# Four key tiles of values at a time: twelve tiles of logits and three buffers of streamed weights

## The chip, the cores and the metric

The kernel runs on one core of a Trainium2 chip. The time is what the device takes for one execution, in microseconds (us), as a median over runs. The engines of the core are named as in the profile: PE is TensorE (matmuls), PEld its weight loads, DVE is VectorE, ACT is ScalarE, POOL is GpSimd, and SP is the engine whose queue issues the DMAs.

## What is computed

The input is x, eight images of 512 channels and 32x32 pixels in float32. Layer 0 is group normalization followed by a block with two attention bottlenecks, added to x; layer 1 is group normalization followed by a 1x1 convolution with a masked weight and a permutation of its channels, added again. Cut to what matters here:

```
t  = silu(bn(conv1x1(gn(x))))                    # 512 -> 512, in two halves of 256
ys = [t[:, :256], t[:, 256:]]
for i in range(2):
    z = silu(bn(conv3x3(ys[-1])))                # 256 -> 256
    q, k, v = conv1x1(z)                         # 4 heads of 64 channels, 1024 pixels
    logits = q^T (k + r) / 8                     # 1024 x 1024 for every head
    z = softmax(logits) v
    z = silu(bn(conv1x1(z)))
    ys.append(ys[-1] + z)
x = x + silu(bn(conv1x1(concat(ys))))            # 1024 -> 512
x = x + permuted_masked_conv1x1(gn(x))           # 512 -> 512
```

All matmuls are in float32. The trace shows two PE instructions for each of them (one for a transpose).

## The kernel before

The attention is cut into 64 **units**: eight images, two bottlenecks, two pairs of heads, two halves of the 1024 queries. Within a unit the 1024 keys lie in eight **key tiles** of 128. For each key tile t a unit does the following steps, which are methods of the class `Unit`:

- `logits(t)` (L487): two matmuls, one for each head of the pair, each into a PSUM bank of its own. Each uses 64 of the 128 rows of the array, so that the two run side by side. ScalarE copies both banks into an SBUF tile `st` of 128x1024 (L500), and VectorE keeps a running maximum `mx` straight from the banks (L505).
- `top` and `spread` (L507, L516): once per unit, transposes on TensorE (`mt`, `mb`) turn the running maximum into the negated maximum of each query, spread over all partitions.
- `soften(t)` (L523): VectorE adds that maximum to `st` (L525), ScalarE takes the exponential in place (L526), GpSimd adds the tile to the running sum of the denominator (L531).
- `values(t)` (L533): two matmuls, one for each head, each into 64 of the 128 columns of the array, again side by side, accumulated over all eight key tiles into one PSUM bank `po` (L537).
- `finish` and `divide` (L545, L554): the denominators (`den`), their reciprocals, and the division of `po` into `q`.

The loop over units (L1003 to L1034) is a software pipeline written out by hand. While a unit's tiles are softened and its values are taken, the logits of the next unit are made. A pass of the inner loop handles two key tiles, t and t+1: soften both, take the values of the two tiles of the pass before, make the next unit's logits of t and t+1, and then let `advance` put in a share of the **filler**, the work of all other stages. The filler of a slot of four units is the 3x3 convolution of a coming bottleneck (`m<-plane`, L297), its projection to q, k and v (`qk`, `v`, L175 and L389), and a background list of 1x1 convolutions (`cv<-x`, `cv<-y`, `l<-x`, `m<-q`, all at L175). Each filler matmul uses the whole 128x128 array. Its results are taken out of PSUM by ScalarE or VectorE. The shares that `advance` hands out are counted in estimated costs, so that the filler falls at the same place of a unit whatever the values do.

What the change and the prediction touch:

- PSUM has eight banks: two for `mb` (pool `ps_m`), one for `po` (`ps_o`), and five (`ps_f`, L63) that logits, filler, `mt` and `den` share. Two key tiles of logits take four of these five.
- The pool `stp` (L53) holds ten tiles `st`: the eight of the unit that is softened and two for the next unit's logits. The logits of the third key tile go where the first tile of the current unit was, so that their copy comes after the values and the sum of that tile.
- `wp` (L54) has four buffers of streamed weights (6 KB a partition each), `wt` (L60) three temporaries of the transform before the 3x3 convolution.
- Nearly all DMAs are issued by the one queue of SP, in an order that the scheduler of the tile framework writes when the kernel is built. It also orders each engine's instructions. VectorE's order of softening, maximum and transform is held by `in_turn` (L182).
- `bn_sb`, `s_sb`, `rw_sb` and `rh_sb` (L86 to L89) hold small parameters, and `tri` (L658) a triangular matrix; each has SBUF of its own.

Of the kernel before, what the change touches and what calls it, by code (L numbers as in the profile page):

```python
# [15 lines left out]
F32 = mybir.dt.float32  # L16
# [6 lines left out]
P = 128  # L23
NB = 8
CT = 4
IT = 2
F = 32
HW = F * F
HALF = 512
NBLK = 2  # L30
HD = 64
NG = 16
KT = 8
NGR = 17

BN_CV1, BN_CV2, BN_M1, BN_M2, BN_ALL = 0, 4, 8, 12, 16
# [3 lines left out]
def conv_preact_kernel(ctx: ExitStack, tc: tile.TileContext, x, cv1, cv2, mcv1, qkv, mcv2, bn, rw, rh, conv, s_in, t_in, out):  # L40
# [3 lines left out]
    def pool(name, bufs, **kw):  # L44
        return ctx.enter_context(tc.tile_pool(name=name, bufs=bufs, **kw))

    const = pool("const", 1)
    dram = pool("dram", 1, space=bass.MemoryType.DRAM)
    small = pool("small", 2)
    qp = pool("qp", 2)  # L50
    kp_ = pool("kvp", 3)
    stp = pool("stp", 10)
    one = pool("one", 1)  # L53
    wp = pool("wp", 4)  # L54
    gx = pool("gx", 4)
    wm = pool("wm", 1)
    gy = pool("gy", 4)
    gr = pool("gr", 2)
    tp = pool("tp", 3)
    wt = pool("wt", 3)  # L60
    ps_m = pool("ps_m", 1, space=PSUM)
    ps_o = pool("ps_o", 1, space=PSUM)
    ps_f = pool("ps_f", 5, space=PSUM)  # L63
# [7 lines left out]
    def half_tile(name):  # L71
        return tp.tile([P, HALF], F32, tag="t", name=name)
# [10 lines left out]
        return t  # L83


    bn_sb = const.tile([P, 4, BN_ALL], F32, name="bn_sb")  # L86
    s_sb = const.tile([P, 2, CT, NG], F32, name="s_sb")
    rw_sb = const.tile([P, NBLK, IT, F], F32, name="rw_sb")
    rh_sb = const.tile([P, NBLK, IT, F], F32, name="rh_sb")  # L89


    w_m1 = [[dram.tile([P, IT, IT, 3, P], F32, name=f"w_m1_{i}_{r}") for r in range(6)] for i in range(NBLK)]
# [515 lines left out]
    def last_weights():  # L608
# [46 lines left out]

        yield

        tri = small.tile([P, P], F32, tag="tri", bufs=1, name="tri")  # L658
        nc.gpsimd.affine_select(
            out=tri, in_=ones, pattern=[[1, P]], compare_op=ALU.is_gt, fill=0.0, base=0, channel_multiplier=-1  # L660
        )
# [28 lines left out]
        for i in range(CT):  # L690
# [5 lines left out]
            t = half_tile(f"wl_{i}")  # L696
# [35 lines left out]
    clock = Clock()  # L732
# [138 lines left out]
    def slot_filler(s):  # L871

        prev = slots[s - 1] if s else (None, 0)
        nxt = slots[s + 1] if s + 1 < len(slots) else (None, 0)
        todo, needed = [], 0.0

        def add(us, g):
            nonlocal needed
            todo.append((us, g))
            needed += us  # L880

        im, i = nxt
        add(8.0, bg.take(8.0))
        if im and i == 1:
            add(7.0, im.conv_m2(0))
            add(0.0, call(im.transform, 1, 3.0, 1.0))
            add(9.0, bg.take(9.0))
        products = im.conv3(i) if im else iter(())
        if prev[1] == 1:
            if im:  # L890
                add(21.3, (us for _, us in zip(range(16), products)))
            add(7.0, prev[0].conv_m2(1))
            add(0.0, call(lambda: finishing(prev[0])))
        if im:
            add(10.7 if prev[1] == 1 else 32.0, products)
            add(7.0, bg.take(7.0))
        if im:
            add(21.0, im.project(i))
        if s + 2 < len(slots) and slots[s + 2][1] == 0:
            add(0.0, call(slots[s + 2][0].load_y))  # L900
            add(0.0, call(slots[s + 2][0].transform, 0, 8.0, 1.3))
        rest = SHARE - needed if im else 70.0
        if rest > 0:
            todo.append((rest, bg.take(rest, wait=True)))
        total = sum(c for c, _ in todo)
        return needed, total, todo
# [36 lines left out]
    first, second = images[:2]  # L943
# [16 lines left out]
    bg.prepare()  # L960
    first.transform(0, 0.0, 0.0)
    side = last_weights()
    for n, us in enumerate(first.conv3(0)):
        clock.tick(us)
# [16 lines left out]
    for s in range(len(slots)):  # L981
        needed, total, todo = slot_filler(s)
        state = {"done": 0.0}

        def filler():
            for us, g in todo:
                start = state["done"]
                for cost in g:
                    clock.tick(cost)
                    state["done"] += cost  # L990
                    yield

                state["done"] = max(state["done"], start + us)

        fill = filler()

        def advance(share):
            goal = max(share * total, min(1.0, share / 0.74) * needed + 0.1)
            while state["done"] < goal:
                if next(fill, "end") == "end":  # L1000
                    break

        steps = 4 * (KT + 2)  # L1003
        for j in range(4):
            u = units[4 * s + j]
            nxt = units[4 * s + j + 1] if 4 * s + j + 1 < len(units) else None
            base = j * (KT + 2)
            u.top()
            clock.tick(0.9)
            advance((base + 1) / steps)  # L1010
            u.spread()
            clock.tick(0.9)
            advance((base + 2) / steps)
            if before:
                before.finish()
                clock.tick(0.9)
            for t in range(0, KT, 2):
                u.soften(t)
                if before and t == 0:
                    before.divide(1)  # L1020
                u.soften(t + 1)
                if t:
                    u.values(t - 2)
                    u.values(t - 1)
                    clock.tick(2.0)
                if nxt:
                    nxt.logits(t)
                    nxt.logits(t + 1)
                    clock.tick(2.0)
                advance((base + 4 + t) / steps)  # L1030
            u.values(KT - 2)
            u.values(KT - 1)
            clock.tick(2.0)
            before = u  # L1034
        for _ in fill:
            pass
# [59 lines left out]
```

## Time and profile before

| what | time |
|---|---|
| median of three runs | 3276.86 us (3268.33 to 3284.32) |
| the profiled execution | 3278.47 us |
| its span, first to last instruction | 3276.7 us |
| PE busy | 3159.1 us, 96% of the span |
| DVE busy | 2045.9 us, 62% |
| ACT busy | 1756.6 us, 54% |
| POOL busy | 1219.1 us, 37% |
| mean granted TensorE clock | 0.990 |

The profiled execution lies 1.61 us above the median, and its span 1.8 us below its own time. A unit takes about 3276.7 / 64 = 51.2 us. A group of instructions in the profile is named by engine, line, the tile written and the tiles read. A matmul's form is given as rows by columns of the array: 128\*128 for the filler, 64\*128 for logits (`lg`), 128\*64 for values (`po`). Matmuls overlap in the pipeline, so that their listed durations are longer than the distance from one start to the next; the distance is what the stream costs. An idle time is put down to the engine whose result ended it.

### The profile page before, as it was taken

Reading aid. Unit: us, or ns where it says so; the run is one execution under the profiler, and the core shown is the slowest. Engines: PE = TensorE matmul, PEld = TensorE weight load, DVE = VectorE, ACT = ScalarE, POOL = GpSimd, SP = SyncE. Lnnn points to the kernel's source line nnn. Section 1 sums busy time; section 2 is a strip of 40 time slices with the busy share of each in tenths; the row PEclk is TensorE's granted clock in tenths of the full one; section 3 lists DMA queues with packets and bytes.
Section 4 is the critical chain, followed back from the end, with each engine's and each line's share of the span. In section 5 each row is a group of like instructions: output and inputs, shape, how many; then the busy total and the mean of one; then the engine's idle time right before and its main releaser. Section 6 shows DMA issues by size and latency. Waiting matters only on the chain.

```text
span 3276.7 us, 33257 instructions
## 1 busy us (share of the span) xinstructions
PE 3159.1 (96%) x11716; PEld 1538.0 (47%) x11716; DVE 2045.9 (62%) x2717; ACT 1756.6 (54%) x2369; POOL 1219.1 (37%) x971
## 2 busy tenths in 40 slices
PE   7999999998999999999999999999999999999998
PEld 3645345353545445354545445354445444453343
DVE  5436566666666575767666675767656676666642
ACT  3245765854545655644545555644655554646631
POOL 2104433335334343344334343444334433444420
PEclk9999999999999999999999999999999999999999
DMA  8752352330323241423323341423333341423366
GB/s 292 275 171 71 119 170 94 116 106 20 121 98 106 75 148 55 161 84 106 122 98 105 104 144 54 161 84 108 124 105 108 101 141 49 160 71 116 111 217 205
DMA packets 142007, 399.30 MB, mean 122 GB/s; under 512 B 13072, under 2 KB 14352, under 8 KB 141840
## 3 DMA queue, kind: packets, MB, share of 16 engines
q1 hardware_dynamic: 141120, 396.94, 36.1%
q8 instruction: 93, 1.52, 0.2%
q14 instruction: 74, 0.61, 0.1%
q10 hardware_dynamic: 720, 0.23, 0.0%
HBM read 317.42 MB, written 79.69 MB: 121 GB/s over the span
## 4 chain that ended last, share of the span: by engine, by line
PE 69%; DVE 11%; issue 5%; ACT 4%; DMA 4%; POOL 1%; POOLq 0%; SPq 0%; ACTq 0%; DVEq 0%
PE cv L175 14%; PE m L297 12%; PE po L537 11%; PE lg L494 10%; PE qk L175 6%; PE l L175 5%; PE v L389 3%; DVE st L525 3%; PE mt L513 2%; PE m L175 2%; DVE rb L556 2%; DVE mx L505 2%; PE den L549 2%; PE mb L521 2%; DMA x<-in_x 1%
## 5 line engine op out<-in xcount | busy, mean ns | idle before, releaser
L531 POOL TENSOR_TENSOR sum<-sum,st 128x512 f32<-128x512 f32 x768 | 973.9, 1299 | 771.5 <-ACT st L526 771.5
L526 ACT ACTIVATE st<-st 128x1024 f32<-128x1024 f32 x512 | 534.3, 1056 | 471.4 <-DVE st L525 464.8
L505 DVE TENSOR_TENSOR mx<-mx,lg 128x512 f32<-128x512 f32 x768 | 479.3, 681 | 434.1 <-ACT st L500 433.6
L500 ACT COPY st<-lg 128x512 f32<-128x512 f32 x1024 | 528.1, 594 | 246.1 <-PE lg L494 189.9
L525 DVE TENSOR_TENSOR st<-st,mb 128x1024 f32<-128x1024 f32 x512 | 604.2, 1213 | 79.8 <-PE mb L521 79.8
L297 PE MATMUL m<-plane,w_m 128*128 128x256 f32 x2304 | 534.0, 386 | 18.0 <-DVE z L351 8.3
L494 PE MATMUL lg<-q,k 64*128 64x512 f32 x2048 | 534.6, 618 | 10.4 <-ACT rb L551 3.3
L537 PE MATMUL po<-st,v 128*64 128x512 f32 x2048 | 509.5, 609 | 17.2 <-ACT st L526 11.4
L297 PEld LDWEIGHTS m<-plane,w_m 128*128 128x128 f32 x2304 | 431.4, 191 | 142.7 <-issue 40.8
L531 POOL TENSOR_TENSOR sum<-st,st 128x512 f32<-128x512 f32 x128 | 162.2, 1288 | 834.1 <-ACT st L526 712.0
L175 PE MATMUL cv<-y,w_cv 128*128 128x512 f32 x1024 | 466.5, 600 | 4.9 <-DVE mx L505 2.1
L494 PEld LDWEIGHTS lg<-q,k 64*128 64x128 f32 x2048 | 188.9, 186 | 346.2 <-issue 236.5
L175 PEld LDWEIGHTS cv<-y,w_cv 128*128 128x128 f32 x1024 | 185.5, 190 | 252.0 <-issue 231.6
L537 PEld LDWEIGHTS po<-st,v 128*64 128x64 f32 x2048 | 125.2, 136 | 327.6 <-issue 231.6
L556 DVE RECIPROCAL rb<-rb 128x256 f32<-128x256 f32 x128 | 216.1, 1725 | 66.0 <-ACT rb L551 66.0
L175 PE MATMUL cv<-x,w_cv 128*128 128x512 f32 x512 | 242.2, 622 | 12.3 <-DVE mx L505 4.1
L175 PE MATMUL l<-x,w_l 128*128 128x512 f32 x512 | 235.2, 604 | 9.6 <-DVE mx L505 6.2
L175 PE MATMUL qk<-z,w_qkv 128*128 128x512 f32 x512 | 234.2, 600 | 1.6 <-DVE mx L505 1.6
L514 DVE TENSOR_REDUCE nm<-mt 128x4 f32<-128x512 f32 x128 | 83.0, 685 | 221.5 <-PE mt L513 221.2
L130 ACT ACT_TABLE_LOAD x122 | 156.5, 1283 | 14.7 <-PE m L175 6.4
L175 PEld LDWEIGHTS cv<-x,w_cv 128*128 128x128 f32 x512 | 97.0, 197 | 138.7 <-issue 112.1
L175 PEld LDWEIGHTS l<-x,w_l 128*128 128x128 f32 x512 | 93.3, 191 | 133.6 <-issue 106.5
(144 smaller groups left out, 2342.1 us busy)
## 6 DMA issues: line engine op xcount, KB each, us to landing
w_m<-w_m SPq DMA_DIRECT2D x96, 768.0 KB, 4.4
w_cv<-in_cv SPq DMA_DIRECT2D x90, 512.0 KB, 3.5
y<-y SPq DMA_DIRECT2D x64, 512.0 KB, 4.7
x<-in_x SPq DMA_DIRECT2D x56, 512.0 KB, 5.2
y<-y SPq DMA_DIRECT2D x64, 256.0 KB, 3.6
k<-r SPq DMA_DIRECT2D x32, 512.0 KB, 3.8
res<-y SPq DMA_DIRECT2D x32, 512.0 KB, 4.2
xr<-in_x SPq DMA_DIRECT2D x32, 512.0 KB, 4.3
```

Of the source, the lines that this page charges most:

```text
L130: nc.scalar.activation(dst, src, AF.Silu, bias=bn_b[:, col : col + 1], scale=bn_s[:, col : col + 1])
L175: nc.tensor.matmul(ps, w, moving, start=(n == 0), stop=(n == len(terms) - 1))
L297: nc.tensor.matmul(ps[:, ts(co, 256)].rearrange("p (t x) -> p t x", x=F), w[:, co, c, dx], u[:, 9 * c : 9 * c + 8, dx : dx + F], start=(j ...
L389: nc.tensor.matmul(ps[:, ts(j, P)], z[:, c, ts(4 * j4 + j, P)], w[:, c, 512 + P * hp : 512 + P * hp + P], start=(c == 0), stop=(c == IT - 1),)
L494: nc.tensor.matmul(lg[h], self.k[r, ts(t, P)], self.q[r, self.hp, ts(self.half, HALF)], start=True, stop=True)
L500: nc.scalar.copy(st[:, h], lg[h])
L505: in_turn(nc.vector.tensor_tensor(self.mx[:, h], so_far[:, h], lg[h], ALU.max))
L525: in_turn(nc.vector.tensor_tensor(st, st, flat(self.mb), ALU.add))
L526: nc.scalar.activation(st, st, AF.Exp)
L531: nc.gpsimd.tensor_tensor(self.acc[:, h], so_far[:, h], self.st[t][:, h], ALU.add)
L537: nc.tensor.matmul(self.po[HD * h : HD * h + HD], self.v[:, t, ts(h, HD)], self.st[t][:, h], start=(t == 0), stop=(t == KT - 1),)
L556: nc.vector.reciprocal(self.rb[:, r], self.rb[:, r])
```

## The change

The values of four key tiles are taken together: tiles 0 to 3 in the pass t = 4, ahead of the next unit's logits of tiles 4 and 5, and tiles 4 to 7 after the last pass. The passes t = 2 and t = 6 have no values. So that the next unit's logits of four key tiles find a place before the first values are taken, `stp` has twelve tiles. The 8 KB come from one weight buffer (`wp` 3), one temporary (`wt` 2), and from the small parameters and `tri`, which now share one buffer of the keys' pool `kvp` at the start. All edits, with blank lines left out:

```diff
-    stp = pool("stp", 10)
+    stp = pool("stp", 12)
-    wp = pool("wp", 4)
+    wp = pool("wp", 3)
-    wt = pool("wt", 3)
+    wt = pool("wt", 2)
...
-    bn_sb = const.tile([P, 4, BN_ALL], F32, name="bn_sb")
-    s_sb = const.tile([P, 2, CT, NG], F32, name="s_sb")
-    rw_sb = const.tile([P, NBLK, IT, F], F32, name="rw_sb")
-    rh_sb = const.tile([P, NBLK, IT, F], F32, name="rh_sb")
+    par = kp_.tile([P, HW], F32, tag="k", name="par")
+    def param(first, shape):
+        return par[:, first : first + P].rearrange("p (a b c) -> p a b c", b=shape[0], c=shape[1])
+    s_sb = param(0, (CT, NG))
+    rw_sb = param(128, (IT, F))
+    rh_sb = param(256, (IT, F))
+    bn_sb = par[:, 512 : 512 + 4 * BN_ALL].rearrange("p (a b) -> p a b", b=BN_ALL)
...
-        tri = small.tile([P, P], F32, tag="tri", bufs=1, name="tri")
+        tri = par[:, 384:512]
...
                 u.soften(t + 1)
-                if t:
-                    u.values(t - 2)
-                    u.values(t - 1)
-                    clock.tick(2.0)
+                if t == KT // 2:
+                    for key in range(KT // 2):
+                        u.values(key)
+                    clock.tick(4.0)
                 if nxt:
                     nxt.logits(t)
                     nxt.logits(t + 1)
                     clock.tick(2.0)
                 advance((base + 4 + t) / steps)
-            u.values(KT - 2)
-            u.values(KT - 1)
-            clock.tick(2.0)
+            for key in range(KT // 2, KT):
+                u.values(key)
+            clock.tick(4.0)
```

## The prediction, on record before the run

> **What bounds the kernel now.** I read the busy table first, then the chain of waits in one unit, then who waited for whom, then VectorE's and SP's timelines around the places that the change moves.
>
> The busy table:
>
> ```profile
> PE 3159.1 (96%) x11716; PEld 1538.0 (47%) x11716; DVE 2045.9 (62%) x2717; ACT 1756.6 (54%) x2369; POOL 1219.1 (37%) x971
> ```
>
> TensorE is nearly always busy, so the time is TensorE's work plus the few waits in it. The change can gain only in what the stream itself costs, or in those waits. The chain of waits in 1224 to 1250 us shows the stream (start, duration, what):
>
> ```profile
> 1224.63 1.87 PE po L537 x8
> 1226.49 1.92 PE lg L494 x8
> 1228.41 5.38 PE m L297 x24
> 1233.79 1.87 PE po L537 x8
> 1235.66 1.92 PE lg L494 x8
> 1237.58 5.38 PE m L297 x24
> 1242.95 1.87 PE po L537 x8
> 1244.82 1.97 PE lg L494 x8
> ...
> 1247.03 0.57 ACT st L500
> ...
> 1247.63 0.70 DVE mx L505
> ...
> 1248.37 1.78 PE m L297 x7
> ```
>
> Two things are to be seen. A group of values (po, two key tiles) takes 1.87 us. Full-array matmuls of 512 columns follow each other every 0.43 us (24 of the kind `cv<-x` run from 152.21 to 162.51 us, 0.429 each), and eight half-array ones, two abreast, fill four such places: 1.72 us. So each group costs 0.15 us for changing the form. And at the end the filler (m at 1248.37) waits for a bank: logits, then ScalarE's copy, then VectorE's maximum. That is the chain which paces TensorE where it waits at all.
>
> Waits of all engines, and TensorE's alone (total us, times, longest):
>
> ```profile
> DVE mx L505 <- ACT st L500: 446.9, 185, 9.2
> ACT st L500 <- PE lg L494: 189.9, 98, 7.3
> ```
>
> ```profile
> PE po L537 <- ACT st L526: 11.4, 6, 4.4
> PE mt L513 <- DVE mx L505: 10.7, 3, 3.6
> ...
> PE po L537 <- DVE q L558: 5.8, 8, 0.9
> ```
>
> ScalarE's copies wait for TensorE's logits only 98 times, of some 256 pairs of key tiles; otherwise ScalarE or VectorE is late and TensorE ahead. TensorE's waits are small because its stream is spaced widely enough. VectorE in the same stretch:
>
> ```profile
> 1237.44 2.48 DVE L505 TENSOR_TENSOR mx<-mx,lg 128x512 f32<-128x512 f32 x4 [4.27 <-ACT st L500]
> ...
> 1243.69 2.34 DVE L525 TENSOR_TENSOR st<-st,mb 128x1024 f32<-128x1024 f32 x2
> 1247.63 2.48 DVE L505 TENSOR_TENSOR mx<-mx,lg 128x512 f32<-128x512 f32 x4 [1.60 <-ACT st L500]
> ```
>
> One pass costs VectorE 2.34 (soften two tiles), 1.60 (last exponential and first copy on ScalarE) and 2.48 (four maxima): 6.4 us in a row, and its filler work on top (here six operations between 1239.84 and 1243.77, 3.9 us). TensorE's pass takes 1.87 + 1.92 + 5.38 = 9.2 us.
>
> **The change, part by part.**
>
> *Form changes removed.* Two groups of four places, joined, lose one 0.15 us (0.14 by the step to the next group within rounding; I take 0.14). Two joints a unit in 64 units would be 128. The order of instructions in the two built programs has 947 changes of form before and 834 after, 113 fewer, because the scheduler still splits some groups. 113 x 0.14 = **-16 us**, all on the path, since TensorE is the path. Ends: 113 x 0.09 (a bare change: 0.52 instead of 0.43 us between starts at a border) = -10, and 128 x 0.15 = -19.
>
> *Logits come earlier in the passes t = 2 and t = 6.* Without the values ahead of them, the next unit's logits of these passes, and the filler behind them, start 1.87 us earlier; TensorE's pass is then 7.3 us, against VectorE's 6.4 plus filler work. What is late next is the five shared banks. In the shown pass, the filler at 1248.37 waits for a bank whose maximum ended at 1248.33. That maximum hangs on the softening at 1243.69, which stands behind VectorE's work for the 3x3 convolution and not behind the logits. Logits at 1242.95 instead of 1244.82 don't free it sooner: TensorE stops for about 1.87 us, and the values that had filled this time are still to be done later. So there the whole 1.87 is lost. In the pass that starts at 1224.63 the filler's next bank was free 0.62 us before its need, and 1.87 - 0.62 = 1.25 is lost.
>
> I did this for all 63 units that have a next one, from the trace's semaphore events: for every TensorE instruction between the group that goes and the next group, how long before its start its last input or bank had come, letting ScalarE and VectorE move up where their own inputs and predecessors permit. What is short of 1.87 us is lost. For t = 2, 43 of 63 units lose, together 49 us; for t = 6, 25 of 63, 35 us. The upper end is +84 us, the lower end 0.
>
> Three things make it less. (a) In the new program ScalarE copies the logits of these passes ahead of the second exponential more often: the third key tile in 36 units instead of 24, the seventh in 16 instead of 5. Each brings the maximum forward by one exponential (1.06 us): 23 x 1.06 = -24 us at best, and I take it. (b) A unit that stopped at t = 2 is later at t = 6 and finds VectorE further on; mean loss 49/63 = 0.8 us, for the some 25 units with a loss at t = 6, in the four tenths of them where the copy does not wait for TensorE at the fifth tile: -7 us. (c) Waits of TensorE elsewhere shrink: values wait for exponentials (11.4), for the division (5.8: the first values now stand one pass later), transposes for the last maximum (10.7). Of these 28 us I take two thirds, -18; ends 0 and -28. Together 84 - 24 - 7 - 18 = **+35 us**.
>
> The copies that waited for the sums of GpSimd (41.3 us, 18 times) and for values (14.4, 7 times) because the tile was not free lose that wait with twelve tiles. ScalarE is not the bound, so I cost this at nothing; the bound is inside (c).
>
> *The rule and the row.* The Trainium skill, page "TensorEngine Tiling (Array Packing)", says in Key Properties that a change of tiling mode drains TensorE, which the 0.15 us show. Its section PSUM Bottleneck says that tiling speeds up the matmuls but not the emptying of PSUM, which speaks against this change. It gives no duration for either. By that rule alone none of the 84 us would come back, and the sum would be 68 us slower.
>
> *Weights in three buffers instead of four.* A load is issued when the buffer comes free, a use later than before. SP's timeline:
>
> ```profile
> 1379.11 0.42 SPq L78 DMA_DIRECT2D w_m<-w_m  x1
> ...
> 1398.57 11.22 SPq L78 DMA_DIRECT2D w_m<-w_m  x2
> ```
>
> The weights issued at 1379.11 are first used at 1409.3. With three buffers, one of them held by a background convolution, they would be issued when the product two before ends, at 1398.5, land some 4.4 us later (the median of these loads) or 7.4 at worst, and still be 3.4 us early. Over all loads the margin before use is 5 us or more with three buffers, outside four places like this one. What stands behind the load on SP's in-order queue moves too: walking the new order of the queue with the old release times, only two weights near 160 us, where TensorE does nothing but filler, land late (3.8 us, one wait), and two image tiles by about 1 us. **+4 us**, ends 0 and +8.
>
> *The rest.* Two temporaries instead of three: all their writers and readers but the last are VectorE's, in order; nothing. The parameters in a buffer of the keys: used only until 160 us, before the third key tile of keys is loaded; nothing. Twelve tiles at the start let weights' raw pieces load earlier, on a stretch where TensorE already runs: nothing.
>
> *Sum.* -16 + 35 + 4 = +23 us on the profiled 3278.5, which is 1.6 above the median: **3300 us** against 3276.9.
>
> **Rivals.**
>
> - *TensorE keeps its pace, faster.* If VectorE, which idles 38% of the span, follows the earlier logits, the losses at t = 2 and t = 6 stay under some 15 us and only -16 and -18 remain: 3250 us or so, at best 3277 - 16 - 28 = 3233. For it: 38 of 63 units have no loss at t = 6. Against it: the copies wait for TensorE in only 98 cases. It decides where the banks' losses, after (a) and (b), are below 18 us.
> - *It cancels, no change.* Losses of 18 to 50 us, against the same gains: 3260 to 3293. One step of mine, (a) or (c), being twice as good suffices.
> - *All is lost.* Nothing of the 84 comes back: 3277 - 16 + 84 + 8 = 3353.
> - *Weights become the bound.* The queue's head waits longer with three buffers and holds up image loads and stores. For it: SP waits mostly for buffers of weights. Against it: margins above. Price: 4 to 5 us for each late load, 30 late loads for 4%; I give it little.
> - *It doesn't do what it says.* The scheduler could split the groups again; the order shows 15 of 128 joints missing, which is counted.
>
> **How the numbers follow.** Measurements of this kernel tell about 0.5% (16 us) from no change. Forecast, slower by over 0.5%, with all-lost and weights: 0.45 + 0.08 + 0.03; cancels 0.24; TensorE keeps its pace 0.20. The range reaches from a little above the best case, 3245, to a little below the worst, 3345; the likeliest case's own range is 3293 to 3325.
>
> **What would show it.** Right: groups of 16 values in a row with 3.58 us or so; fewer form changes; TensorE's waits for `mx` (filler after the third and seventh logits) up by some 40 us, those of values for exponentials down; the waits of copies for GpSimd's sums gone. Wrong: if waits for `mx` don't grow, VectorE followed; if waits for DMAs appear on PE, the weights were the matter; if the busy share of VectorE's chain moves forward by more than an exponential, my static margins were too strict.

## The result, and the profile after

The changed kernel takes 3289.75 us (median of nine runs, 3282.92 to 3301.72), against 3277.7 us for the kernel before on the same chip. The ratio is 1.0038, with a 95% interval of 1.0022 to 1.0053: slower by 0.38%, some 12 us. The profiled execution took 3292.98 us, with a span of 3291.0 us.

The busy table after:

```profile
PE 3168.4 (96%) x11716; PEld 1550.7 (47%) x11716; DVE 2036.6 (62%) x2717; ACT 1757.5 (53%) x2371; POOL 1217.1 (37%) x971
```

TensorE is still the path, with the same number of instructions and more time. The chain of waits around the same work as before (the middle of a 3x3 convolution):

```profile
1227.58 6.67 PE m L303 x30
1234.25 1.92 PE lg L500 x8
1236.17 1.49 PE m L303 x6
...
1237.68 4.15 PE m L303 x18
1241.83 3.58 PE po L543 x16
1245.41 1.11 PE lg L500 x4
...
1253.53 2.26 DVE st L531 x2
1255.79 0.61 DVE mx L511
...
1256.45 4.15 PE m L303 x18
```

The joint is there: 16 values in a row take 3.58 us, where two groups took 2 x 1.87 = 3.74. What a joint saves is some 0.15 us. And the chain leaves TensorE for longer before the filler at 1256.45 gets its bank: from 1246.52 to 1256.45, almost all of it on VectorE (the maximum of the logits before, filler work, softening, the next maximum), where before it left TensorE for 1.6 us. Such a stretch is not lost as a whole: TensorE had other work meanwhile and stood idle for 0.32 us of it. TensorE's own waits, and ScalarE's for TensorE:

```profile
PE cv L181 <- DVE mx L511: 10.3, 11, 4.3
PE m L303 <- DVE mx L511: 9.3, 12, 2.6
PE lg L500 <- DVE mx L511: 9.1, 12, 1.3
PE l L181 <- DVE mx L511: 7.3, 7, 1.2
PE cv L181 <- DMA w_cv<-in_cv: 6.2, 1, 6.2
...
PE po L543 <- ACT st L532: 5.0, 4, 2.3
```

```profile
ACT st L506 <- PE lg L500: 241.9, 124, 5.7
```

Waits for the running maximum (mx), which holds a bank, have grown at the filler and the logits: from 20 waits with 21.9 us to 49 with 40.8. The transposes' wait for it (10.7 us before) is gone from the list, the values wait less for exponentials (5.0 instead of 11.4), and ScalarE now waits for logits 124 times instead of 98. ScalarE's wait for GpSimd's sums is nearly gone (1.0 us, 41.3 before).

To sum this up I split every distance from one TensorE start to the next in the trace: the **place** that the first matmul takes (0.43 us for 512 columns, 0.215 for 256, 0.11 for 128), where two half-array matmuls that start within 0.1 us share one place; the cost of **changes of form** (up to 0.1 us at a border, and what is under 0.13 us for the first matmuls behind it); and **waits**, the rest. The sums in us, for the profiled executions of before and after and of those experiments below that need them:

| kernel | full-array places | half-array places | form | waits | sum |
|---|---|---|---|---|---|
| before | 1973.7 | 983.8 | 162.9 | 135.9 | 3256.3 |
| after | 1973.7 | 1006.6 | 144.8 | 145.7 | 3270.9 |
| mem | 1973.7 | 988.5 | 158.9 | 135.7 | 3256.8 |
| uneven | 1973.7 | 1007.0 | 165.3 | 153.3 | 3299.3 |
| even | 1973.7 | 1006.4 | 142.6 | 124.4 | 3247.1 |
| rows | 1973.7 | 991.9 | 134.5 | 182.2 | 3282.3 |
| even12b | 1973.7 | 996.8 | 127.2 | 136.2 | 3233.9 |

After against before: form -18.1, waits +9.8, and half-array places +22.8, which nobody had asked for. 102 more instructions of logits or values than before started without their partner, which makes 51 more places of 0.43 us. 22 of these places belong to the logits of the fourth key tile, 23 to the values of the first and the fourth. TensorE's timeline shows a case of logits:

```profile
1319.64 1.12 PE L500 MATMUL lg<-q,k 64*128 64x512 f32 x2
1321.07 1.12 PE L500 MATMUL lg<-q,k 64*128 64x512 f32 x2 [0.31 <-ACT st L506]
```

Two instructions are one head. The second head's bank came late, so the two heads ran one after the other, where four instructions side by side need 0.86 us. It is the rule for the fourth key tile: in each of the 21 units where its pair is torn, the last wait of the second head ended after the first head had started, by the semaphore events of the trace.

The values are torn in another way. Their two heads share one bank, and no late bank parts them; in TensorE's instruction order, which the scheduler writes, other work stands between the two heads of the first key tile:

```profile
251.29 1.07 PE L543 MATMUL po<-st,v 128*64 128x512 f32 x2
253.80 5.45 PE L303 MATMUL m<-plane,w_m 128*128 128x256 f32 x24 [1.44 <-ACT y L136]
259.18 3.65 PE L543 MATMUL po<-st,v 128*64 128x512 f32 x14
```

One head of the first tile runs alone, its partner behind 24 filler instructions, and at the end of the row one head of the fourth tile is left alone too.

### The profile page after: what moved, and what is told of

Its sections match the earlier page's. It is cut to its first block, busy times and chain, and to the rows that moved or that the text cites. A ratio compares the mean times of both kernels' runs of the same rounds, so it can differ in the third digit from the quotient of the medians.

```text
span 3291.0 us, 33235 instructions
## 1 busy us (share of the span) xinstructions
PE 3168.4 (96%) x11716; PEld 1550.7 (47%) x11716; DVE 2036.6 (62%) x2717; ACT 1757.5 (53%) x2371; POOL 1217.1 (37%) x971
## 4 chain that ended last, share of the span: by engine, by line
PE 63%; DVE 16%; issue 6%; ACT 5%; DMA 3%; POOL 0%; SPq 0%; ACTq 0%; POOLq 0%; DVEq 0%
PE cv L181 12%; PE po L543 11%; PE m L303 11%; PE lg L500 8%; PE qk L181 6%; PE l L181 4%; DVE st L531 4%; DVE rb L562 3%; PE v L395 3%; DVE mx L511 3%; PE mt L519 2%; PE mb L527 2%; PE m L181 2%; PE den L555 2%; ACT st L532 1%
## 5 line engine op out<-in xcount | busy, mean ns | idle before, releaser
L500 PE MATMUL lg<-q,k 64*128 64x512 f32 x2048 | 545.0, 619 | 17.2 <-DVE mx L511 9.1
L543 PE MATMUL po<-st,v 128*64 128x512 f32 x2048 | 495.7, 604 | 6.4 <-ACT st L532 5.0
L543 PEld LDWEIGHTS po<-st,v 128*64 128x64 f32 x2048 | 138.3, 137 | 317.5 <-issue 283.6
```

What stands on the lines that cost most here:

```text
L500: nc.tensor.matmul(lg[h], self.k[r, ts(t, P)], self.q[r, self.hp, ts(self.half, HALF)], start=True, stop=True)
L543: nc.tensor.matmul(self.po[HD * h : HD * h + HD], self.v[:, t, ts(h, HD)], self.st[t][:, h], start=(t == 0), stop=(t == KT - 1),)
```

## The experiments

The theory: the next unit's logits of the passes t = 2 and t = 6 come 1.87 us too early for the five banks that VectorE and ScalarE empty, and this costs more than the changes of form bring. The rivals: the memory parts (three weight buffers, SP's queue) cost it; or the pairs of heads that the scheduler tears apart. Ratios are to the kernel before, timed on the same chip in five rounds.

**mem.** The changed kernel with the old loop over values:

```diff
-                if t == KT // 2:
-                    for key in range(KT // 2):
-                        u.values(key)
-                    clock.tick(4.0)
+                if t:
+                    u.values(t - 2)
+                    u.values(t - 1)
+                    clock.tick(2.0)
```

and the same at the unit's end.

> The memory parts alone: twelve tiles, three weight buffers, two temporaries, shared parameters, but the values of two key tiles at a time as before. If the new order of values makes the loss, this stands within 0.2% of before (3270 to 3284 us), with one wait of some 6 us for weights near 160 us and without the waits of ScalarE's copies for GpSimd's sums. If the memory parts make it, it is slower by 0.3 to 0.4% like the changed kernel, and the waits of TensorE for DMAs or VectorE grow as there.

Measured 0.9998 (0.9989 to 1.0008). The one wait for weights is there (6.0 us), as expected; the waits of copies for GpSimd's sums are down from 41.3 to 5.8 us, where I had expected none:

```profile
PE cv L181 <- DMA w_cv<-in_cv: 6.0, 1, 6.0
```

Twelve tiles, three weight buffers, two temporaries and the shared parameters together change nothing that can be measured. The memory parts are not the cause.

**even.** The changed kernel with filler moved, so that the logits are spaced as before:

```diff
-                advance((base + 4 + t) / steps)
+                advance((base + 4 + t + (0.72 if t % 4 == 0 else 0.0)) / steps)
```

> The changed kernel with 1.87 us of filler moved from the passes t = 2 and t = 6 to the passes t = 0 and t = 4 (0.72 of a step), so that the next unit's logits of every two key tiles follow each other as far apart as before. If the early logits make the loss, the waits and the lonely half-array matmuls at the fourth key tile (8.8 us and 22 x 0.43 us more than before) go, the filler's waits stay in part, and it takes 3260 to 3278 us. If the loss is from the memory parts or from pairs of heads that the scheduler tears apart, it stays at 3285 to 3295.

Measured 0.9958 (0.9945 to 0.9971): 0.8% less than the changed kernel, and faster than before. Its waits are 124.4 us, 21.3 less than in the changed kernel. But the lonely half-array matmuls did not go, although I had expected it: the logits of the fourth key tile fell from 154 places to 142 (128 would be needed if no pair were torn), others rose (the eighth from 131 to 148), and the sum stayed at 1006.4 us. So restoring the distance takes away waits, and lonely matmuls remain.

**uneven.** The mirror: the kernel before, values in twos, with filler moved so that the third and seventh tiles' logits are early:

```diff
-                advance((base + 4 + t) / steps)
+                advance((base + 4 + t + (-0.72 if t % 4 == 0 else 0.0)) / steps)
```

> The kernel before, values in twos, with the filler shifted the other way: 1.87 us of it taken from the passes t = 0 and t = 4 and put into t = 2 and t = 6, so that the third and the seventh key tiles' logits come 1.87 us earlier, as in the changed kernel. If early logits are what costs, this is slower by 15 to 40 us (3295 to 3320) with the waits and the lonely half-array matmuls at the fourth key tile. If the loss comes from taking the values in fours, it stays within 8 us of before.

Measured 1.0128 (1.0114 to 1.0141), slower by 42 us, a little more than expected, with no change of values at all. Places rose by 23.2 and waits by 17.4, the two terms that rose in the changed kernel. They did not rise by the same waits, though: those for mx at the filler and the logits went only from 21.9 to 26.7 us. The others that grew are the logits' own waits (26.5 us in all instead of 10.4, most of them for ScalarE) and those of values for exponentials; ScalarE's copies also wait for tiles that values still hold:

```profile
PE po L537 <- ACT st L526: 19.7, 11, 3.0
```

```profile
ACT st L500 <- PE po L537: 47.0, 15, 7.4
```

These four kernels are a square. The mean distance between the starts of the logits of tiles 0 and 2, 2 and 4, 4 and 6 is 8.35, 10.35, 9.83 us in before and 8.97, 9.86, 9.53 in even; it is 6.46, 13.13, 7.65 in uneven and 6.97, 12.24, 7.74 in the changed kernel. At about equal distances values in fours are faster than in twos: 0.9958 at the even ones, and 1.0038 / 1.0128 = 0.991 at the uneven ones. At equal values the uneven distances cost 1.28% in twos and 1.0038 / 0.9958 = 0.80% in fours. The change did both, and the second outweighed the first.

**even0 and even4.** The filler moved in one half of the unit only: `0.72 if t == 0` and `0.72 if t == 4`.

> The changed kernel with filler moved only from the pass t = 2 to t = 0. By the margins of the trace before (49 us at t = 2, 35 at t = 6) it keeps six tenths of the gain of moving both, 24 us: some 14 us less than the changed kernel, 3275. If the changed kernel's own waits at the fourth key tile are the whole of it, it keeps nearly all: 3266 to 3270.

> The changed kernel with filler moved only from the pass t = 6 to t = 4. By the margins of the trace before, four tenths of the 24 us: 3280. If the waits at the fourth key tile are the whole of it, nothing: 3287 to 3291.

Measured 1.0007 (0.9995 to 1.0018) and 0.9991 (0.9982 to 1.0000). The two gains, 0.31% and 0.47% against the changed kernel, add up to that of both (0.80%). Both passes cost, so the fourth key tile is not the whole of it. But the shares are the other way round: six tenths lie at t = 6 and four at t = 2, where the margins of the trace before had said the opposite. The two intervals overlap a little, so this order is likely and not certain.

**rows.** The changed kernel with TensorE's order held around the values (all matmuls go through this helper, values with `keep=True`):

```diff
+    last_pe = [None, False]
+    def in_row(i, keep=False):
+        if last_pe[0] is not None and (keep or last_pe[1]):
+            tc.add_manual_dep(i.ins, last_pe[0], IN_ORDER, reason="order of TensorE")
+        last_pe[:] = i.ins.name, keep
+        return i
```

> The changed kernel with TensorE's order around the values held as written, so that no pair of heads is torn apart (25 pairs of values in the changed kernel, 8 before) and all values of four key tiles stand in one row. If torn pairs make most of the loss, it gains 25 x 0.86 us and some form changes (56 fewer, 0.15 us each), about 25 us: 3262 to 3272 us. If the early logits make it, the gain is below 15 us, since tiles held in a row wait where the torn ones let other work pass: 3275 to 3290.

Measured 1.0080 (1.0067 to 1.0094): slower still, by 0.42%. It missed both ranges. Held in order, the half-array places fell by 14.7 us and form by 10.3, as the sum has it, but waits rose by 36.5:

```profile
PE lg L74 <- DVE mx L525: 20.1, 13, 6.1
...
PE m L74 <- DVE mx L525: 18.6, 16, 2.3
PE cv L74 <- DVE mx L525: 14.3, 11, 4.3
```

I read it so that torn pairs of values are how the scheduler lets other work pass a late input, a symptom of the early logits. What is shown is only that mending them alone makes this kernel slower.

**even_rows.** Both edits together.

> Both edits: filler moved and TensorE's order around the values held. If the two causes are separate, their gains add: 3245 to 3265 us, faster than before. If one is the other's symptom, it is no better than the better of the two alone.

Measured 1.0043 (1.0028 to 1.0057). The gains don't add: holding the order costs 0.85% on top of the even spacing. Here the logits are not early, so that the reading of torn pairs as their symptom does not explain it. Why it costs as much, although the spacing is that of before, these runs leave open.

**before_rows.** The same helper in the kernel before.

> The kernel before with TensorE's order around the values held as written; 32 changes of form fewer and 8 torn pairs mended, worth 32 x 0.15 + 8 x 0.86 = 12 us if nothing waits: 3268. If holding the order costs by letting nothing pass a wait, as it did with values in fours (17 us slower than without), it is slower than before: 3285 to 3300.

Measured 0.9969 (0.9956 to 0.9982), faster, as the sum without waits has it (-10 us against -12). So held order is no loss by itself in twos. That the sizes agree is in part luck: the trace has 43 fewer places of logits and values, 27 of them of logits, which the sum did not hold.

**late.** The kernel before, values in twos, with the edit of even:

> The kernel before, values in twos, with 1.87 us of filler moved from the passes t = 2 and t = 6 to t = 0 and t = 4, as in the faster variant with values in fours. If the gain there is the removed changes of form with the spacing restored, this one, whose spacing becomes uneven the other way, is no faster than before: 3276 to 3295. If the place of the filler alone makes the gain, it is faster by 0.3 to 0.5%: 3264 to 3271.

Measured 0.9966 (0.9952 to 0.9980): the second of the two outcomes. The place of the filler is worth as much in twos as the fours are at even spacing. The old place of the filler was therefore not the best one for either, and a gain of even over before must not be read as the worth of the fours alone: with the same edit of the filler in both, even stands to late as 0.9958 to 0.9966, within their intervals. late also tells what costs: its distances are 10.63, 8.02 and 11.61 us, no more even than those of before. So uneven distances as such do not cost; early logits of the third and the seventh tile do.

**even12, even18, even12b.** More filler moved: 1.2, 1.8, and 1.2 at t = 0 with 1.8 at t = 4.

> The changed kernel with 3.1 us of filler moved (1.2 of a step) instead of 1.87. The logits of the third and seventh tiles then come later than before; if their banks were still late in places, the rest of those waits goes and it takes 3258 to 3265 us; if the even spacing was already the best, the shorter passes t = 2 and t = 6 make values and transposes wait for VectorE and it takes 3266 to 3275.

> Values in fours with 1.8 of a step (4.7 us) of filler moved, which leaves the passes t = 2 and t = 6 nearly without filler. The order has 718 changes of form instead of 791 at 1.2 and 829 at 0.72, since some filler between values and logits is gone; 73 fewer at 0.15 us are 11 us. If nothing else changes: 3252 to 3256. If logits of the pass before and after then come too close and wait for banks: 3265 to 3285.

> Values in fours with 1.2 of a step moved at t = 0 and 1.8 at t = 4; 758 changes of form. Between the two neighbours where they differ by place alone: 3255 to 3265; clearly outside of them if one of the two passes has another optimum.

Measured 0.9950 (0.9937 to 0.9964), 0.9965 (0.9951 to 0.9979) and 0.9928 (0.9914 to 0.9942). even12 stands in the first of its two ranges, even18 in the second. even12 has distances near those of late (10.20, 8.35 and 11.04 us) and differs from it by less than their intervals, so that a gain of the fours is not shown at this spacing. even12b is faster than both its neighbours and just below its range, which fits a best place of its own for each of the two passes. It is the fastest of all, 3254.19 us against 3277.81 for before. Its chain of waits stays on TensorE over a whole unit:

```profile
1205.59 9.27 PE m L303 x42
1214.86 2.35 PE lg L500 x7
1217.21 2.79 PE m L303 x12
1220.00 3.58 PE po L543 x16
1223.58 1.92 PE lg L500 x8
1225.50 10.56 PE m L303 x48
1236.06 1.92 PE lg L500 x8
1237.98 3.58 PE po L543 x16
1241.56 1.02 PE mt L519 x8
```

The filler between the fifth and the seventh tile is 10.56 us, and behind the seventh nothing stands between logits and values. There a change of form is saved besides (758 in the order, 834 in the changed kernel), and the table has 17.6 us less for form than the changed kernel. even18 has still fewer changes and is slower than even12b. Its logits of tiles 2 and 4 are 6.48 us apart, against 8.33 in even12b, and it has 153.7 us of waits in the same split; that this closeness is the reason is read from the trace and was not tested further. In twos only 1.87 us of filler were moved, so that the worth of the fours with the best place of the filler for each is not shown.

## Why the prediction was right, and where a term was off

The forecast was 3300 us, 0.7% slower; measured is 0.38% slower, within the range and on the forecast's side, but inside the 0.5% that it called no change. By size it is thus the rival "it cancels" (3260 to 3293) that came, and not the likeliest case (3293 to 3325). Of the signs named ahead, the rows of 16, the fewer changes of form, the shorter waits of values and the end of the copies' waits for GpSimd came; the waits for mx rose by 18.9 us at the filler and the logits, not by some 40.

- *Form changes removed*, -16 us: right. The trace has 951 changes of form before and 838 after, 113 fewer as in the order, and the split has -18.1 us.
- *Logits come earlier*, +84 us before reliefs: the mechanism was right. uneven shows it without the fours, and even shows it by undoing it. Net of the three reliefs +35 us was forecast; the profiles have +9.8 of waits and +22.8 of lonely half-array matmuls, +32.6. But I had looked for all of it in waits for banks. Two thirds of the net came as heads that lost their partner, a term that I didn't have. For the 22 places of the fourth tile's logits the cause is the one I had, late banks; the 23 of the values come from the instruction order, which I had not looked at for this. That the two sums agree so well is therefore in part luck.
- *(a), copies ahead of the exponential*, -24 us: the mechanism was right, and the trace has the copies ahead in the 36 and 16 units of the order. In the one place I compared it brought more than the one exponential that I had priced: at the same convolution, the wait that I had put at the whole 1.87 us came out at 0.32, because one copy ran before the exponentials. TensorE's and ScalarE's timelines after:

```profile
1256.45 1.78 PE L303 MATMUL m<-plane,w_m 128*128 128x256 f32 x7 [0.32 <-DVE mx L511]
```

```profile
1253.88 0.58 ACT L506 COPY st<-lg 128x512 f32<-128x512 f32 x1 [5.24 <-PE lg L500]
1254.70 1.06 ACT L532 ACTIVATE st<-st 128x1024 f32<-128x1024 f32 x1 [0.23 <-DVE st L531]
```

  VectorE's maximum could follow its softening at once (2.26 and 0.61 in the chain above, without the 1.60 us of before). Its sum over the kernel was not measured by itself.
- *(b), a stop at t = 2 makes t = 6 later*, -7 us (8 by its own figures): not measured by itself.
- *The two passes' losses*, 49 us at t = 2 and 35 at t = 6: mis-sized. even0 and even4 give 0.31% and 0.47%, 10 and 15 us. The margins were static and did not know which units' order the scheduler would change; that this is the reason was not tested.
- *(c), waits elsewhere*, -18 us: right. In the split, waits at the transposes fell by 11.4 us and those of the values from 20.8 to 11.1 us, together -21.
- *Weights in three buffers*, +4 us: the one late load is there (6.2 us in after, 6.0 in mem) and, as forecast, no others of weight; but in mem other waits shrank as much, and the sum is zero.

The term that made the forecast too high by some 11 us is thus the net of the early logits together with the weights: +39 in the sum. By time, the square has 26 us (0.80%) in its place, and -14 us (0.42%) for the fours at even spacing, where the sum had -16.

The rival "TensorE keeps its pace" fell with the time itself and with uneven: VectorE and ScalarE did not follow. "Weights become the bound" and the memory parts fell with mem.

## What to carry to other kernels

In a software pipeline whose busiest engine feeds others through a few shared buffers, joining work of that engine also moves everything between the joined pieces; move filler into the gap so that producers of shared banks keep their distance, and tune that place again. Here joining lost 0.4% as it stood and gained 0.35 to 0.7% on the kernel before once 2 to 5 us of filler had been moved; a move of 2 us brought 0.3% without the joining. When you price a change by its waits, count also the pairs that run side by side: when one partner's buffer is late, or the instruction order puts other work between the two, each takes a place of its own, and no row of waits shows it.

## What the runs showed of the hardware that was not expected

Two half-array matmuls shared a place of 0.43 us only where they could start at once. Where the second waited for its bank (1319.64 and 1321.07 above), or stood behind other work in the order (251.29 and 259.18), each took its own place. 51 such places, 22 us, separate after from before, and they count as busy time: PE's busy sum rose from 3159.1 to 3168.4 us although its work was the same and it changed its form less often.
